# A two-layer attention and feed-forward kernel: the last block's normalised input transposed by DMA, its weights loaded once, exponentials written to PSUM

## The chip, the cores and the metric

The kernel runs on one core of a Trainium2 chip. The metric is the device time of one execution in microseconds. Before the change the median of three runs is 1620.17 us (1619.24 to 1620.29). A core has five engines that run their own instruction streams and meet at semaphores: TensorE (PE), VectorE (DVE), ScalarE (ACT), GpSimd (POOL) and SyncE (SP), which here only issues DMAs. Data lives in SBUF (128 partitions) and in eight PSUM banks that TensorE writes.

## The reference

There are 32 batches; each has x and a context of 128 rows by 1024. Four blocks are added to x one after the other:

```python
x = x + _L0_xattn_ref(_layernorm(x), ctx, ctx)      # autocorrelation through FFTs, top 9 of 128 lags, softmax
x = x + _L0_ffn_ref(_layernorm(x), W_base, ...)     # 1024x1024 base product + 8 LoRA experts of rank 16, top 2
x = x + _L1_xattn_ref(_layernorm(x), ctx, ...)      # 8 heads over a sliding window of 16
x = x + _L1_ffn_ref(_layernorm(x), A, B, Wr)        # 4 LoRA experts of rank 16, top 2, no base product
```

The fourth block, which the change touches most, is

```python
logits = flat @ Wr.T
topk_vals, topk_idx = jax.lax.top_k(logits, 2)
gates = softmax(logits where they are in the top 2, else -inf)
mid = jnp.einsum('tf,erf->ter', flat, A)
delta = jnp.sum(gates[:, :, None] * jnp.einsum('ter,eor->teo', mid, B) * 4.0, axis=1)
```

## The kernel before

**Stages.** `mk_kernel` walks over the 32 batches (line 964). For each it calls `load_batch` (stage `load`), `autocorr` for each half of 512 columns (stages `spec`, `corr`, `top`, `wt`, `inv`), `ffn0` (`ffn0`, `gate`, `base`), `attention` (`kv`, `q`, `S`, `PV`, `wo`) and `ffn1`. A stage works on tiles of 128 x 512 fp32 in SBUF (`U()`, 43 buffers named `u`) and on PSUM banks of the same shape (`B()`, eight named `p`). Products that need more than 16 bits take each operand as a pair of fp16 numbers, high part and remainder, and sum three matmuls (`THREE`, line 429); `pair(U())` holds such a pair in one `u` buffer.

**The fourth block before.** `ffn1` (line 932) calls `ln`, which takes mean and variance from row sums that `wo` left (`stats`: two squares on ACT, a power on POOL) and returns `normalise(g)`, one activation from x to a new `u` buffer. `transposed` (line 787) turns the normalised half with four TensorE transposes of 128 x 128 fp32 into a PSUM bank. An ACT activation writes the high fp16 part of it, a DVE subtraction the remainder. Twelve matmuls per half against `ar4` (128 x 68) give the low-rank product and the router's logits. `ffn0` uses `transposed` in the same way and keeps it.

**Weights.** `prep_ffn` scales every weight by its largest absolute value. For the base weights, before took a bound in its place: it loaded the 16 pieces of 128 x 512, multiplied each 128 x 128 part with itself on TensorE, summed all in one bank, took the sum of the diagonal and its square root on POOL. Then it loaded the 16 pieces a second time (`load_w`) and `pieces` made the pairs `wsp`, in turns by "P" (high part on POOL, remainder on DVE) and "V" (high part on ACT, remainder on DVE).

**The softmax of the lags.** In `autocorr` the correlations stand in a PSUM bank `pc`. Four activations (lines 758 and 759) write exp(pc - max) to a `u` buffer; a DVE instruction keeps the top 9 of each row.

**What sets the order.** Nothing is issued as it is called. `Planner` records each operation (a group of matmuls is one), works out what depends on what through its tiles, and estimates a duration (`_cost`). `plan` then places the operations one by one on the five engines: whenever an engine is free in the plan's own clock, the ready operation with the lowest value of `T * batch - tail - bias[stage]` goes next, where `tail` is the estimated work that hangs on it. Buffers are handed out in that order; a bound on how many batches are open (`win`), reserves of buffers (`su`, `sp`, `ru`, `rp`) and `margin` hold operations back. `emit` writes the instructions out in the planned order, so that every engine's order is fixed in the program, and on the chip an engine waits at an instruction until its operands are there. All instructions therefore carry one line in the profile, L363, and are told apart by their tiles. A DMA's semaphore is one of eight that SP uses in turn; SP waits for the DMA eight before.

Of the kernel before, what the change touches and what calls it, by code (L numbers as in the profile page):

```python
# [27 lines left out]
TINY = 1e-30  # L28
CFG = {'nu': 43, 'nd': 2, 'en': 'G', 'cl': 'G', 'xl': 'G', 'sm': 'V', 'sw': 'A', 'wg': 'PV', 'gram': 1, 'q0': 'G', 'ns': 28, 'nt': 48, 'phases': ((0.0, {'T': 19.75, 'margin': 43, 'win': 5, 'su': 4, 'sp': 0, 'ru': 1, 'rp': 0, 'bias': {'kv': -4.7, 'load': 9.8, 'S': -5.8, 'gate': 42.6, 'ffn1': 24.9, 'q': 1.0, 'top': 0.7, 'PV': -5.5, 'inv': 3.0, 'wt': 9.9, 'spec': 6.0, 'wo': 18.7, 'ws': -16.0, 'base': -2.4, 'ffn0': 56.2, 'corr': 7.7, 'setup': -2.3}}),)}
NTOP = int(2 * math.log(S))  # L30
# [75 lines left out]
class Planner:  # L106
# [72 lines left out]
    def _cost(self, op, method, v, kw):  # L179
# [27 lines left out]
        elif eng == "DVE":  # L207
            n = max(n, size(src))
            two = method in ("tensor_copy", "tensor_scalar", "memset") and not psum and n > 64
            op.dur += 6 * n / 0.96 + 67 if method == "reciprocal" else (n * (0.5 if two else 1.0) + 64 + 59 * nsc) / 0.96  # L210
            op.dur += 70.0 * ("accum_out" in v) + {"match_replace": 67.0, "transpose": 25.0}.get(method, 0.0)
        elif eng == "Pool":
            small = mybir.dt.size(out.proto.dtype) == 2
            if method == "memset":
                op.dur += 40.0 + (0.85 if small else 0.2) * n
            else:
                rate = 1.2 if method == "tensor_scalar" else 1.88 if small else 2.1
                if any(x.proto.ap[-1][0] == 0 for x in v.values()) and n > 128:
# [14 lines left out]

    def plan(self, phases, stop=None):

# [11 lines left out]
        for t in tiles:  # L247
            t.index = None
        for o in reversed(ops):
            o.tail = o.dur + max((s.tail + self._lat(o, s) for s in o.succs  # L250
                                  if s.batch == o.batch or o.batch < 0 and s.batch <= 0), default=0.0)
# [24 lines left out]
        while events:  # L276
            now = events[0][0]
            if stop is not None and now > stop:
                break
            if phases and now >= phases[0][0]:  # L280
# [3 lines left out]
            while events and events[0][0] <= now:  # L284
# [14 lines left out]
                for s in o.succs:  # L299
                    s.ready = max(s.ready, now + self._lat(o, s))  # L300
                    s.wait -= 1
# [8 lines left out]
            for e in self.ENGINES:  # L310
                if busy[e] > now:
                    continue
                for i, (_, o) in enumerate(ready[e]):
# [17 lines left out]
                    order.append(o)  # L331
                    end = now + o.dur
                    busy[e] = now + o.cold if e == "SP" else end
# [18 lines left out]
        self.order = order  # L352
        if stop is None and len(order) < len(ops):
            return None
        return now

# [8 lines left out]

def plan_args(c):
    scarce = lambda f: {"u": f["su"], "p": f["sp"], "d": 9, "m": 3, "r": 9, "s": 9, "t": 9}
    reserve = lambda f: {"u": f["ru"], "p": f["rp"], "m": 1, "s": 4, "t": 6}
    return [(t * 1e3, (f["T"] * 1e3, f["win"], f["margin"] * 1e3, scarce(f), reserve(f),
                       {k: v * 1e3 for k, v in f["bias"].items()})) for t, f in c["phases"]]  # L370


@with_exitstack
def mk_kernel(ctx: ExitStack, tc: tile.TileContext, T: dict, out: bass.AP):
# [23 lines left out]
    def U():  # L398
        return P.tile("u")
# [39 lines left out]
    G.memset(mhalf, -0.5)  # L439
    half = const("half", [128, 1])  # L440
    G.memset(half, 0.5)

# [79 lines left out]
    def prep_ffn():  # L522
        mx, m5 = P.fixed(slot("wmx", [128, 32])), P.fixed(slot("wm5", [128, 5]))
        absmax = lambda o, i, ax=AX.X: V.tensor_reduce(o, i, axis=ax, op=ALU.max, apply_absolute_value=True)

        def load_w(k):
            t = U()
            SP.dma_start(out=t, in_=T["wbT"][k // 2 * 128 : (k // 2 + 1) * 128, k % 2 * HALF : (k % 2 + 1) * HALF])
            return t

        def load_ar(name, i, w, rows):
# [15 lines left out]
        if CFG["gram"]:  # L547

            V.scalar_tensor_tensor(M(), p[:, 0:128], 1.0, ident, op0=ALU.mult, op1=ALU.mult, accum_out=mx[:, 1:2])
            V.tensor_scalar(mx[:, 2:3], mx[:, 1:2], TINY, None, op0=ALU.add)  # L550
            G.tensor_tensor(mx[:, 0:1], mx[:, 2:3], half, op=ALU.pow)
        for i in range(4):
# [7 lines left out]
        for i, (lo, hi) in enumerate(((0, 1 if CFG["gram"] else 16), (16, 20), (20, 24), (24, 26), (26, 28))):  # L560
            V.tensor_reduce(m5[:, i : i + 1], mx[:, lo:hi], axis=AX.X, op=ALU.max)
# [83 lines left out]
    def ln(src, sums):  # L645
# [10 lines left out]
        return normalise  # L656

    def gates(vals, E, pex, tl, sc, fac, imm):

# [67 lines left out]
    def autocorr(b, hf, normalise, x, c16, ksc, sums):  # L727
# [236 lines left out]
    for b in range(NB):  # L964
# [7 lines left out]
        ffn1(b, x, sums)  # L972
    P.plan(plan_args(CFG))
    with tc.manual_schedule():
# [79 lines left out]
```

## Time and profile before

| | us |
|---|---|
| median of three runs | 1620.17 |
| profiled execution | 1620.67 |
| its span | 1618.9 |
| PE busy | 1539.9 |
| DVE busy | 1467.7 |
| ACT busy | 1407.4 |
| POOL busy | 1369.9 |
| DMA queue q1, share of 16 engines | 49.5% |

The profiled execution's time is its span, from the first instruction to the last, and 1.8 us around it. Busy times are sums over an engine's instructions, and a row of the profile reads: engine, operation, output <- inputs by tile name, shape, count, then busy time and the mean duration of one in nanoseconds, then the engine's idle time just before such instructions and who ended it. The mean of one matmul is longer than its share of the engine, because matmuls overlap; busy time over count is nearer to what one costs. From about 600 to 1450 us the profile repeats itself batch by batch.

### The profile page before, as it was taken

What the parts mean: (1) busy time and instruction counts of PE and PEld (TensorE: products, weight loads), DVE (VectorE), ACT (ScalarE), POOL (GpSimd) and SP (SyncE); (2) the same over time, 40 slices, a digit from 0 to 9 for tenths busy, and PEclk for the clock granted to TensorE, in tenths of its full rate; (3) what the DMA queues carried; (4) which work ended last, traced back from release to release, by engine and by line L of the source; (5) the groups of instructions that cost most, each with busy time, mean ns of one, the idle gap of its engine ahead of it and who ended that gap; (6) DMA issues with size and microseconds to landing.
All of it is one profiled execution on the core that took longest, in us unless ns stands there. A gap on an engine that the chain in (4) does not pass through costs nothing.

```text
span 1618.9 us, 52341 instructions
## 1 busy us (share of the span) xinstructions
PE 1539.9 (95%) x19272; PEld 1012.6 (63%) x19272; DVE 1467.7 (91%) x5037; ACT 1407.4 (87%) x2817; POOL 1369.9 (85%) x1508
## 2 busy tenths in 40 slices
PE   5589999999999999999999999999999999999974
PEld 4345666666666666666666666666666666666653
DVE  5978999999999999999999999999999999999774
ACT  5698989998999989999999999999999999998752
POOL 6888879899798898988889998888899888889741
PEclk9889999999999999999999999999999999999986
DMA  7713545554554545544455555455555445554441
GB/s 248 216 47 46 91 76 98 92 101 79 107 97 65 96 94 99 96 97 92 65 95 93 100 98 96 91 73 86 95 99 104 89 90 80 79 98 71 64 59 42
DMA packets 856928, 149.96 MB, mean 93 GB/s; under 512 B 808480, under 2 KB 810784, under 8 KB 856672
## 3 DMA queue, kind: packets, MB, share of 16 engines
q1 hardware_dynamic: 856672, 146.61, 49.5%
q8 instruction: 153, 2.51, 0.7%
q14 instruction: 103, 0.84, 0.2%
HBM read 45.99 MB, written 16.78 MB: 39 GB/s over the span
## 4 chain that ended last, share of the span: by engine, by line
PE 58%; ACT 19%; DVE 8%; POOL 6%; issue 6%; DMA 2%; SPq 0%; ACTq 0%; POOLq 0%; DVEq 0%
PE p L363 58%; ACT u L363 17%; DVE u L363 5%; POOL vpad L363 3%; POOL u L363 2%; DVE s L363 2%; DMA u<-in_wbT 1%; POOL t L363 1%; ACT vpad L363 1%; DVE t L363 1%; DVE wsp L363 1%; DVE mm L363 1%; SPq L363 0%; ACT p L363 0%; DMA u<-u 0%
## 5 line engine op out<-in xcount | busy, mean ns | idle before, releaser
L363 POOL TENSOR_TENSOR u<-u,u 128x512 f32<-128x512 f32 (+1 forms) x640 | 772.0, 1234 | 122.7 <-ACT u L363 114.9
L363 PE MATMUL p<-wsp,u 128*128 128x512 f16 (+1 forms) x2304 | 408.7, 327 | 1.7 <-DVE u L363 0.9
L363 ACT ACTIVATE u<-p 64x512 f32<-64x512 f32 (+1 forms) x576 | 328.6, 589 | 73.9 <-PE p L363 62.3
L363 ACT ACTIVATE u<-p,t 128x128 f32<-128x128 f32 (+4 forms) x704 | 335.4, 532 | 34.6 <-PE p L363 21.2
L363 ACT ACTIVATE u<-u,t 128x512 f32<-128x512 f32 (+1 forms) x448 | 312.2, 721 | 39.9 <-DVE u L363 16.6
L363 PEld LDWEIGHTS <-u 128*128 128x128 f16 x3072 | 220.7, 98 | 175.5 <-issue 4.0
L363 DVE SCALAR_TENSOR_TENSOR u<-p,u 128x512 f32<-128x512 f32 (+1 forms) x448 | 291.1, 677 | 37.6 <-PE p L363 24.3
L363 PE MATMUL p<-u,ch 128*128 128x512 f16 x960 | 237.5, 380 | 0.4 <-DVE u L363 0.4
L363 PEld LDWEIGHTS <-qbd 128*128 128x128 f16 x6144 | 173.6, 96 | 29.4 <-issue 10.8
L363 PEld LDWEIGHTS <-vbd 128*128 128x128 f16 x6144 | 164.7, 97 | 31.1 <-issue 27.0
L363 PE MATMUL p<-u,vbd 128*128 128x32 f16 x6144 | 166.3, 177 | 11.4 <-ACT u L363 7.8
L363 PE MATMUL p<-k,qbd 128*128 128x32 f16 x6144 | 175.0, 177 | 0.4 <-issue 0.4
L363 ACT ACTIVATE u<-u,t,t 128x512 f32<-128x512 f32 x192 | 146.8, 815 | 20.4 <-POOL t L363 12.4
L363 PEld LDWEIGHTS <-ch 128*128 128x128 f16 x960 | 90.7, 100 | 102.9 <-issue 13.6
L363 PE MATMUL p<-ident,u 128*128 128x128 f32 x768 | 107.3, 280 | 30.7 <-ACT u L363 25.7
L363 POOL TENSOR_TENSOR u<-u,s 128x512 f32<-128x512 f32 x128 | 133.1, 1051 | 1.0
L363 ACT ACTIVATE u<-u 128x512 f16<-128x512 f32 x194 | 116.1, 628 | 13.1 <-DVE u L363 9.3
L363 PEld LDWEIGHTS p<-ident,u 128*128 128x128 f32 x768 | 87.9, 142 | 59.5 <-ACT u L363 40.6
L363 PE MATMUL p<-u,cf 128*128 128x512 f32 x256 | 119.1, 603 | 0.7 <-POOL u L363 0.7
L363 DVE SCALAR_TENSOR_TENSOR u<-p,t,u 128x256 f32<-128x256 f32 (+1 forms) x192 | 103.6, 555 | 13.7 <-ACT u L363 13.0
L363 POOL TENSOR_TENSOR vpad<-u,vpad 128x512 f16<-128x512 f32 x64 | 100.5, 1575 | 10.1 <-ACT vpad L363 10.0
L363 POOL TENSOR_TENSOR t<-t,mhalf 128x1 f32<-128x1 f32 x128 | 73.0, 571 | 40.8 <-DVE t L363 40.6
(160 smaller groups left out, 2818.5 us busy)
## 6 DMA issues: line engine op xcount, KB each, us to landing
vbd<-d SPq DMA_DIRECT2D x256, 128.0 KB
u<-u SPq DMA_DIRECT2D x192, 128.0 KB
u<-in_ctx SPq DMA_DIRECT2D x64, 256.0 KB
u<-in_x SPq DMA_DIRECT2D x64, 256.0 KB
qbd<-u SPq DMA_DIRECT2D x512, 32.0 KB
out<-u SPq DMA_DIRECT2D x64, 256.0 KB
u<-in_wbT SPq DMA_DIRECT2D x32, 256.0 KB
u<-u SPq DMA_DIRECT2D x64, 126.0 KB
```

The lines of the kernel that those rows point to most:

```text
L363: fn(*[f(a) for a in args], **{k: f(a) for k, a in kw.items()})
```

## The change

`ffn1` no longer transposes on TensorE. A new function `turned` takes the statistics, computes the normalised half twice on ACT (once in fp32, once as the high fp16 part), subtracts them on POOL to the remainder, and `turn` issues one DMA in transposing mode from SP for the pair: 128 x 1024 fp16 in SBUF to eight turned 128 x 128 blocks in another `u` buffer, which the twelve matmuls of that half read. `prep_ffn` loads the base weights once, keeps the 16 buffers, takes the largest absolute values on DVE, and splits them by "V" and "G" (high part and a scaled fp32 copy on ACT, remainder on POOL) in turns. In `autocorr` the exponentials overwrite `pc` in PSUM. The planner's settings are new: other priorities and reserves, a second set of them from 1447 us of the plan's clock on, and a constant added to each DMA's estimated duration; POOL's cost of a scaling with 16-bit output is estimated higher. With these the order of nearly all instructions changes.

```diff
-CFG = {... 'wg': 'PV', 'gram': 1, 'q0': 'G', 'ns': 28, 'nt': 48, 'phases': ((0.0, {'T': 19.75, 'margin': 43, 'win': 5, 'su': 4, 'sp': 0, 'ru': 1, 'rp': 0, 'bias': {...}}),)}
+CFG = {... 'wg': 'VG', 'q0': 'G', 'ns': 28, 'nt': 48, 'plan': {'phases': [{'at': 0.0, 'T': 21.78, 'margin': 26, 'win': 5, 'su': 10, 'sp': 99, 'ru': 1, 'rp': 0, 'bias': {...}}, {'at': 1447.0, 'T': 22.55, 'margin': 20, 'win': 6, 'su': 6, 'sp': 99, 'ru': 3, 'rp': 0, 'bias': {...}}], 'slack': [1.0, 0, 274.653]}}
...
-                rate = 1.2 if method == "tensor_scalar" else 1.88 if small else 2.1
+                rate = (2.8 if small else 1.2) if method == "tensor_scalar" else 1.88 if small else 2.1
...
+        stretch, wait, land = slack
+        lat = lambda a, b: self._lat(a, b) + (wait if a.eng != b.eng else 0.0)
+        dur = lambda o: o.dur if o.eng == "PE" else o.dur + (land if o.batch >= 0 else 0.0) if o.eng == "SP" else o.dur * stretch
...
-        p = B()
+        wb = []
         for k in range(16):
-            t = load_w(k)
-            if not CFG["gram"]:
-                absmax(mx[:, k : k + 1], t)
-                continue
-            with P.group():
-                for j in range(4):
-                    c = t[:, j * 128 : (j + 1) * 128]
-                    PE.matmul(p[:, 0:128], lhsT=c, rhs=c, start=k == 0 and j == 0, stop=k == 15 and j == 3)
...
+            t = U()
+            SP.dma_start(out=t, in_=T["wbT"][k // 2 * 128 : (k // 2 + 1) * 128, k % 2 * HALF : (k % 2 + 1) * HALF])
+            absmax(mx[:, k : k + 1], t)
+            wb.append(t)
...
-            pieces([wsp[:, r, k // 2, lo : lo + HALF] for r in range(2)], load_w(k), 0, CFG["wg"][k % len(CFG["wg"])])
+            pieces([wsp[:, r, k // 2, lo : lo + HALF] for r in range(2)], wb[k], 0, CFG["wg"][k % len(CFG["wg"])])
...
+    def turned(src, sums):
+
+        nm, rs = stats(src, sums)
+        r32, nb = s(1), s(1)
+        G.tensor_scalar(r32, rs, 32.0 * X_SC, None, op0=ALU.mult)
+        G.tensor_tensor(nb, nm, r32, op=ALU.mult)
+
+        def half(g):
+            xn, t, tT = U(), pair(U()), pair(U())
+            A.activation(xn, src[g], AF.Identity, bias=nb, scale=r32)
+            A.activation(t[:, 0], src[g], AF.Identity, bias=nb, scale=r32)
+            G.tensor_tensor(t[:, 1], xn, t[:, 0], op=ALU.subtract)
+            turn(tT, t)
+            return tT
+
+        return half
...
+    def turn(dst, src):
+
+        SP.dma_start(out=dst.rearrange("p i (j n) -> p (i j) n", n=128), in_=src.rearrange("p i n -> p (i n)"), transpose=True)
...
+        for j in range(4):
+            A.activation(pcv[:, j, :], pcv[:, j, :], AF.Exp, bias=nm[:, j : j + 1])
         e = U().rearrange("p (j t) -> p j t", t=128)
-        for j in range(4):
-            A.activation(e[:, j, :], pcv[:, j, :], AF.Exp, bias=nm[:, j : j + 1])
-        V.scalar_tensor_tensor(e, r1, NEG, e, op0=ALU.is_equal, op1=ALU.mult)
+        V.scalar_tensor_tensor(e, r1, NEG, pcv, op0=ALU.is_equal, op1=ALU.mult)
...
-        normalise, ph = ln(x, sums), B()
-        for g in range(2):
-            p, t16 = transposed(normalise, g), pair(U())
-            A.activation(t16[:, 0], p, AF.Copy, scale=32.0 * X_SC)
-            V.scalar_tensor_tensor(t16[:, 1], p, 32.0 * X_SC, t16[:, 0], op0=ALU.mult, op1=ALU.subtract)
+        half, ph = turned(x, sums), B()
+        for g in range(2):
+            t16 = half(g)
```

More of the change, by code (lines that the diff above doesn't have):

```diff
@@ L28 @@
 TINY = 1e-30
-CFG = {'nu': 43, 'nd': 2, 'en': 'G', 'cl': 'G', 'xl': 'G', 'sm': 'V', 'sw': 'A', 'wg': 'PV', 'gram': 1, 'q0': 'G', 'ns': 28, 'nt': 48, 'phases': ((0.0, {'T': 19.75, 'margin': 43, 'win': 5, 'su': 4, 'sp': 0, 'ru': 1, 'rp': 0, 'bias': {'kv': -4.7, 'load': 9.8, 'S': -5.8, 'gate': 42.6, 'ffn1': 24.9, 'q': 1.0, 'top': 0.7, 'PV': -5.5, 'inv': 3.0, 'wt': 9.9, 'spec': 6.0, 'wo': 18.7, 'ws': -16.0, 'base': -2.4, 'ffn0': 56.2, 'corr': 7.7, 'setup': -2.3}}),)}
+CFG = {'nu': 43, 'nd': 2, 'en': 'G', 'cl': 'G', 'xl': 'G', 'sm': 'V', 'sw': 'A', 'wg': 'VG', 'q0': 'G', 'ns': 28, 'nt': 48, 'plan': {'phases': [{'at': 0.0, 'T': 21.78, 'margin': 26, 'win': 5, 'su': 10, 'sp': 99, 'ru': 1, 'rp': 0, 'bias': {'kv': -25.3, 'load': 11.2, 'S': -5.0, 'gate': 236.5, 'ffn1': 51.9, 'q': 45.5, 'top': 0.2, 'PV': -10.3, 'inv': 3.1, 'wt': 15.3, 'spec': 11.1, 'wo': 137.4, 'ws': -5.6, 'base': -3.1, 'ffn0': 59.0, 'corr': 1.3, 'setup': 18.5}}, {'at': 1447.0, 'T': 22.55, 'margin': 20, 'win': 6, 'su': 6, 'sp': 99, 'ru': 3, 'rp': 0, 'bias': {'kv': -38.3, 'load': 17.0, 'S': -7.4, 'gate': 291.2, 'ffn1': 41.4, 'q': 59.7, 'top': 12.3, 'PV': -5.2, 'inv': 29.0, 'wt': 4.4, 'spec': -20.3, 'wo': 151.8, 'ws': 6.4, 'base': -1.8, 'ffn0': 82.1, 'corr': 7.6, 'setup': -12.8}}], 'slack': [1.0, 0, 274.653]}}
 NTOP = int(2 * math.log(S))
@@ L232, in _lat, with plan @@
         return self.LAT[a.eng] + (120.0 if b.eng == "PE" else 0.0)
-    def plan(self, phases, stop=None):
+    def plan(self, phases, slack):
         ops, tiles = self.ops, {}
@@ L248, in plan @@
             t.index = None
+        stretch, wait, land = slack
+        lat = lambda a, b: self._lat(a, b) + (wait if a.eng != b.eng else 0.0)
+        dur = lambda o: o.dur if o.eng == "PE" else o.dur + (land if o.batch >= 0 else 0.0) if o.eng == "SP" else o.dur * stretch
         for o in reversed(ops):
-            o.tail = o.dur + max((s.tail + self._lat(o, s) for s in o.succs
+            o.tail = dur(o) + max((s.tail + lat(o, s) for s in o.succs
                                   if s.batch == o.batch or o.batch < 0 and s.batch <= 0), default=0.0)
@@ L277, in plan @@
             now = events[0][0]
-            if stop is not None and now > stop:
-                break
             if phases and now >= phases[0][0]:
@@ L299, in plan @@
                 for s in o.succs:
-                    s.ready = max(s.ready, now + self._lat(o, s))
+                    s.ready = max(s.ready, now + lat(o, s))
                     s.wait -= 1
@@ L331, in plan @@
                     order.append(o)
-                    end = now + o.dur
+                    end = now + dur(o)
                     busy[e] = now + o.cold if e == "SP" else end
@@ L352, in plan @@
         self.order = order
-        if stop is None and len(order) < len(ops):
-            return None
-        return now
+        return now if len(order) == len(ops) else None
     def emit(self):
@@ L366, in plan_args @@
 def plan_args(c):
+    us = lambda v: v * 1e3
     scarce = lambda f: {"u": f["su"], "p": f["sp"], "d": 9, "m": 3, "r": 9, "s": 9, "t": 9}
     reserve = lambda f: {"u": f["ru"], "p": f["rp"], "m": 1, "s": 4, "t": 6}
-    return [(t * 1e3, (f["T"] * 1e3, f["win"], f["margin"] * 1e3, scarce(f), reserve(f),
-                       {k: v * 1e3 for k, v in f["bias"].items()})) for t, f in c["phases"]]
+    return [(us(f["at"]), (us(f["T"]), f["win"], us(f["margin"]), scarce(f), reserve(f),
+                           {k: us(v) for k, v in f["bias"].items()})) for f in c["phases"]], c["slack"]
 @with_exitstack
@@ L439, in mk_kernel @@
     G.memset(mhalf, -0.5)
-    half = const("half", [128, 1])
-    G.memset(half, 0.5)
     ch = load("ch", dt=F16).rearrange("p (m i n) -> p m i n", m=4, i=2)
@@ L524, in prep_ffn @@
         absmax = lambda o, i, ax=AX.X: V.tensor_reduce(o, i, axis=ax, op=ALU.max, apply_absolute_value=True)
[L526 to L529, printed above, removed]
         def load_ar(name, i, w, rows):
@@ L534, in load_ar @@
             return t
-        p = B()
+        wb = []
         for k in range(16):
-            t = load_w(k)
-            if not CFG["gram"]:
-                absmax(mx[:, k : k + 1], t)
-                continue
-            with P.group():
-                for j in range(4):
-                    c = t[:, j * 128 : (j + 1) * 128]
-                    PE.matmul(p[:, 0:128], lhsT=c, rhs=c, start=k == 0 and j == 0, stop=k == 15 and j == 3)
[L547 to L551, printed above, removed]
+            t = U()
+            SP.dma_start(out=t, in_=T["wbT"][k // 2 * 128 : (k // 2 + 1) * 128, k % 2 * HALF : (k % 2 + 1) * HALF])
+            absmax(mx[:, k : k + 1], t)
+            wb.append(t)
         for i in range(4):
@@ L559, in prep_ffn @@
             absmax(mx[:, 26 + i : 27 + i], t[:, :, 64:68], AX.XY)
-        for i, (lo, hi) in enumerate(((0, 1 if CFG["gram"] else 16), (16, 20), (20, 24), (24, 26), (26, 28))):
+        for i, (lo, hi) in enumerate(((0, 16), (16, 20), (20, 24), (24, 26), (26, 28))):
             V.tensor_reduce(m5[:, i : i + 1], mx[:, lo:hi], axis=AX.X, op=ALU.max)
@@ L972, in mk_kernel @@
         ffn1(b, x, sums)
-    P.plan(plan_args(CFG))
+    P.plan(*plan_args(CFG["plan"]))
     with tc.manual_schedule():
```

## The prediction

> **What bounds the kernel now.** I read the page's totals first, then the busy time in windows of one batch, then the chain of waits inside one window, and then the instruction rows that the change touches.
>
> ```profile
> PE 1539.9 (95%) x19272; PEld 1012.6 (63%) x19272; DVE 1467.7 (91%) x5037; ACT 1407.4 (87%) x2817; POOL 1369.9 (85%) x1508
> ```
>
> TensorE is the fullest, but the other three stand within 11% of it, so the average alone does not say what a gain on TensorE is worth. The windows (length; busy time of PE, PEld, DVE, ACT, POOL; granted clock; DMA share; GB/s) say more:
>
> ```profile
> 0.00:47.00 47.00, 30.03 (x190) 25.56 (x191) 29.17 (x121) 29.80 (x55) 31.28 (x45) 0.93 0.74 234
> 47.00:94.00 47.00, 25.16 (x118) 13.52 (x117) 43.94 (x144) 30.11 (x63) 37.47 (x36) 0.75 0.56 171
> ...
> 840.45:887.50 47.05, 46.90 (x599) 30.63 (x599) 44.31 (x156) 43.18 (x88) 42.05 (x47) 1.00 0.53 91
> ```
>
> In the middle one batch takes 47.05 us and PE works 46.90 of it: there TensorE's own work is the time. The start loses 39 us of PE in 94; the stretch from 1502.7 to the end, asked in the same way, has 87.0 of PE in 116.2. The chain of waits repeats every 47.05 us, and it crosses from the matmuls through DVE, ACT and POOL back to a transpose of `ffn1`:
>
> ```profile
> 840.45 27.25 PE p L363 x308
> ...
> 887.49 0.33 PE p L363
> ```
>
> PE's instructions in order of time:
>
> ```profile
> 84.90 1.12 PE L363 MATMUL p<-ident,u 128*128 128x128 f32 x4 [15.94 <-ACT u L363]
> ...
> 879.60 1.02 PE L363 MATMUL p<-u,woT 128*128 128x512 f32 x2
> ...
> 887.49 0.33 PE L363 MATMUL p<-ident,u 128*128 128x128 f32 x1 [0.15 <-ACT u L363]
> ```
>
> The second product with `woT` at 879.60 gives the row sums that `ffn1` needs; its first transpose starts 7.89 us later, having waited 0.15 us for the normalised x. This chain is the one to watch. The rows whose prices I use:
>
> ```profile
> L363 PE MATMUL p<-ident,u 128*128 128x128 f32 x768 | 107.3, 280 | 30.7 <-ACT u L363 25.7 <-POOL u L363 3.0
> ...
> L363 POOL TENSOR_TENSOR u<-u,u 128x512 f16<-128x512 f32 x256 | 293.1, 1163 | 101.9 <-ACT u L363 101.5
> ...
> L363 ACT ACTIVATE u<-u,t,t 128x512 f32<-128x512 f32 x192 | 146.8, 815 | 20.4 <-POOL t L363 12.4 <-DVE wmx L363 6.2 <-DVE t L363 1.6
> ...
> L363 ACT ACTIVATE u<-p 128x512 f16<-128x512 f32 x192 | 102.1, 586 | 4.1 <-PE p L363 3.2
> ```
>
> **Transposes off TensorE.** 8 of a batch's 24 go. In the same list eight of them start at 870.10 and the next matmul at 870.97, 0.87 us later, 0.109 us each; busy time over count is 0.140. 256 of them are 27.9 to 35.8 us of PE; I take 0.112, the value nearest the dense middle: -28.7 us, 0.9 a batch.
>
> **Where their work goes.** ACT loses the PSUM eviction (102.1/192 = 0.53 us) and gains a second normalisation from SBUF (146.8/192 = 0.76): +0.47 us a batch. DVE loses two subtractions from PSUM (their row: 121.3 us busy for 192, 0.63 each): -1.3. POOL gains two, fp16 out (293.1/256 = 1.145), and one scaling of a column (about 0.2): +2.5. One batch in the middle then asks for PE 46.0, POOL 44.5, ACT 43.7, DVE 43.0. PE stays longest, but its lead over the next falls from 2.6 to 1.5 us.
>
> **The transposing DMA.** No row of before shows one, so I bound how long it takes (L, issue to usable) and count how much time the order gives it. In the order of the built program PE has, between `wo`'s second product of batch b and the first `ffn1` matmul of b: that product 0.86, eight products with `cf` 1.78, eight transposes 0.87, three products of `spec` 0.65, two `S` groups 2.86, two `gate` groups 1.42, five `base` groups of 1.29 and one transpose: 15.0 us. The chain needs 7.9 us to the first normalised half (above), 0.2 for the extra POOL column, 0.8 for the second normalisation, 1.16 for POOL's subtraction: 10.1. So the first DMA has 4.9 us. The second half comes 1.6 us later by ACT and is read one `base` group and twelve matmuls (1.66 us) later: also 4.9.
> L from below: four 128 KB copies `u<-u` and the eight small `qbd` copies are issued on SP at these rates,
>
> ```profile
> 866.81 6.11 SPq L363 DMA_DIRECT2D qbd<-u  x8
> ...
> 873.22 2.48 SPq L363 DMA_DIRECT2D u<-u  x4
> ```
>
> and in the chain of waits of the start:
>
> ```profile
> 23.29 4.25 DMA u<-u
> ```
>
> Two thirds of that (an estimate for the quiet middle) is the low end, 2.8 us. The high end takes the 256 KB as runs of 32 bytes, as `qbd` is written: 32 KB each 0.76 us, so 6.1 us, plus about 2 for a first landing: 8. I take 4.3, at the `u<-u` row, since source rows are 2 KB as there: in time with 0.6 to spare. Past 4.9 every microsecond is paid once a batch, because `wo`, the chain and `ffn1` form a loop through PE's order: about 29 us per us of L. As L may now and then exceed its share I enter +3 us.
>
> The Trainium skill speaks against the move: "VectorE: DVE Perf Modes", sections on the three transpose paths and the rules, prices a 128x128 16-bit transpose at 390 ns on TensorE and 1309 ns by DMA, and says to use TensorE where PSUM will do. Eight such blocks would be an estimated 10.5 us, 5.6 too late, and the sum about 1765. "DMA: Bandwidth & Descriptors", "Latency and other measured facts", gives 261 GB/s for a transposing DMA, by which 256 KB move in an estimated 1.0 us and the sum is the one below. No run here shows either yet.
>
> **SP's queue.** Per batch SP issues 38 DMAs, whose issue times in that window add up to some 29 of 47 us; two more, priced like `u<-u` or `qbd` (0.6 to 0.8 us), are 1.5. Behind the first transpose's wait for POOL stand six `qbd` copies of the next batch, and `S` reads those. Cost taken: nothing, covered by the 18 us that SP has free; if one issue took 3 us instead, the `qbd` copies would come 4.5 us late and `S` would wait some 2 us a batch, 60 in all.
>
> **The start.** Sixteen loads of 256 KB and 64 products of the sum of squares (17.9 us of PE, which stands idle there anyway) go; 16 maxima on DVE (0.66) come, 8 fewer fp16 subtractions on DVE (15.7/16 = 0.98), 16 more activations (0.70). The wait of 15.94 us at 84.90 covers the second loading and splitting; I expect half of it to go. Against this, the new order puts more ACT work early: summing rows over the order, ahead of batch 0's first `ffn1` matmul stand ACT 149.5, POOL 146.3, DVE 145.0, PE 110.6 us, where before had 135.7, 144.8, 142.4 and 128.7. That matmul ran at 188.0, 43.2 after the largest sum. After: 149.5 + 43.2 - 8 = 185 (175 to 195).
>
> **Exponentials in PSUM.** 256 activations now write PSUM. Their row is 0.381 us; the PSUM-to-PSUM rows of 8 and 4 columns (0.318, 0.344) neither forbid a change nor give one: -0.05 to +0.05 each, 13 us of ACT either way over the run, not on the path while ACT has 2 us free a batch. DVE's product reads PSUM, 0.680 for 0.747. The bank is held one DVE step longer, but two banks a batch are no longer taken by transposes. Taken as nothing.
>
> **End.** In the last batch the step from normalised x to the first `ffn1` matmul ran 1605.67 to 1608.20, 2.5 us; now 0.8 + 1.16 + 4.3 = 6.3 less a waiting transpose: +3.
>
> **The sum,** against the profiled execution (1620.67 us, its span 1618.9 and 1.8 around it; 0.5 above the median 1620.17). After batch 0's `ffn1`, before had 1373.9 us of PE work in 1430.9; the new order has 1349.5, 24.4 less. Span: 185 + 1430.9 - 24.4 + 3 (end) + 3 (late DMAs) + 4 (the thinner lead over POOL, 0.3%) = 1601.5; with the 1.8, 1603 us, 1.1% faster.
>
> **Rivals.**
> 1. The DMA comes late, L over 4.9. For it: no row shows one, it waits behind two `qbd` copies, and 8192 short writes are eight `qbd`s. Against: the plain copies of its size land in time. L = 6.5 costs 1.6 x 29 = 46: 1649; L = 8 costs 90: 1693. It passes no change at L = 5.5.
> 2. POOL or ACT becomes the bound. For: POOL at 44.5 of 46.0 with two subtractions that must sit at the right places. Against: DVE ran 44.3 beside PE's 46.9 without costing PE more than 0.15. If PE loses 0.6 a batch: 1620.
> 3. The new order is worse at the start: 16 of 43 `u` buffers hold weights until the scale is known, and more ACT work stands early. 20 us lost there instead of 3 gained: 1626.
>
> **Chances.** Forecast 0.57, rival 1 0.27, rival 2 0.08, rival 3 0.08. The forecast's own range is 1583 to 1617. Under 1580 needs the whole 15.94 us hole and no late DMA; over 1665 needs L over 7, about a third of rival 1: low 1580, high 1665. Below 0.2% (3.2 us) this kernel can't be told from no change: faster 0.59 (forecast, a little of rival 2), same 0.07, slower 0.34.
>
> **What will show it.** One batch in the middle near 46.1 us with PE 45.9 busy; no wait of PE on a DMA of `u` before the `ar` matmuls; if that wait appears, its length times 29 is the loss. POOL near 1445, ACT 1433, DVE 1427 busy. The first `ffn1` matmul near 185. An issue of the transpose on SP above 1 us, or `S` waiting for `qbd`, would show the queue. The prediction is wrong if L exceeds 5.5 or the start loses more than 20.

## The result and the profile after

The changed kernel takes 1626.26 us (median of six runs, 1623.01 to 1628.76), the one before 1619.91 in the same comparison: 1.0036 times as long, with a 95% interval of 1.0023 to 1.0049. It is slower, by 0.36%, where 1.1% faster was forecast. The profiled execution took 1626.28 us, its span 1624.5.

The page's totals, the three windows of the prediction and its row of `ident` transposes, now of the kernel after:

```profile
PE 1515.3 (93%) x18888; PEld 967.5 (60%) x18888; DVE 1447.9 (89%) x4978; ACT 1443.0 (89%) x2833; POOL 1429.8 (88%) x1602
```

```profile
0.00:47.00 47.00, 14.45 (x46) 8.20 (x46) 35.18 (x145) 23.51 (x46) 27.09 (x43) 0.79 0.72 226
47.00:94.00 47.00, 35.15 (x152) 17.16 (x152) 42.19 (x121) 45.64 (x87) 39.83 (x38) 0.85 0.37 107
900.00:947.00 47.00, 46.62 (x604) 30.10 (x601) 44.16 (x154) 44.15 (x88) 43.84 (x50) 1.00 0.58 103
```

```profile
L363 PE MATMUL p<-ident,u 128*128 128x128 f32 x512 | 80.6, 280 | 7.5 <-ACT u L363 4.9 <-POOL u L363 2.2
```

The instructions have moved as the diff says: 8 of 24 transposes a batch are gone from TensorE, whose busy time fell by 24.6 us. The time did not follow. To see where it went I compare the 16 middle batches of both kernels (from the first `ar` matmul of batch 10 to that of batch 26; the columns are those of the windows above), before first:

```profile
655.12:1408.27 753.15, 750.73 (x9570) 490.49 (x9569) 708.98 (x2481) 690.53 (x1393) 672.83 (x736) 1.00 0.51 91
```

```profile
654.35:1410.75 756.40, 743.40 (x9441) 478.19 (x9440) 702.75 (x2449) 706.77 (x1393) 701.27 (x785) 1.00 0.57 102
```

A batch went from 753.15/16 = 47.07 us to 47.28, while PE's work in it went from 46.92 to 46.46. Before, PE was idle for 2.4 us in 16 batches; after, for 13.0. The row of the `ar` matmuls, asked for these 16 batches alone, names what it was idle for (behind the second bar: idle time before them, and what ended it):

```profile
L363 PE MATMUL p<-ar,u 128*128 128x68 f16 x384 | 17.4, 195 | 11.5 <-DMA u<-u 11.3
```

The chain of waits through one batch of the kernel after begins and ends with that DMA:

```profile
936.55 4.46 DMA u<-u
...
941.05 25.99 PE p L363 x333
...
983.28 5.81 DMA u<-u
```

PE's and then SP's instructions in order of time around it show which of the two halves is late, and why:

```profile
923.20 1.02 PE L363 MATMUL p<-u,woT 128*128 128x512 f32 x2
...
938.93 0.54 PE L363 MATMUL p<-ar,u 128*128 128x68 f16 x12
939.31 1.46 PE L363 MATMUL p<-wsp,u 128*128 128x512 f16 x6
941.05 0.55 PE L363 MATMUL p<-ar,u 128*128 128x68 f16 x12 [0.29 <-DMA u<-u]
```

```profile
932.46 1.38 SPq L363 DMA_DIRECT2D qbd<-u  x2
934.14 1.36 SPq L363 DMA_TRANSPOSE u<-u  x1
935.55 0.91 SPq L363 DMA_DIRECT2D qbd<-u  x1
936.55 1.54 SPq L363 DMA_TRANSPOSE u<-u  x1
```

The first half (938.93) runs without a wait; the second, one `base` group later, waits. Its DMA could be issued only after SP had spent 1.36 us on issuing the first and 0.91 on a `qbd` copy that stands between them. Over the whole run the first halves wait 0.5 us in sum before the last batch, the second halves 24.2 (added up from the starts of PE's instructions). Issue times on SP (min/median/max in ns) and, in the list of DMAs, the median time from issue to landing (the trace gives a landing for 31 of the 64, nearly all of them second halves):

```profile
L363 SPq DMA_TRANSPOSE u<-u x64: 1242/1433/2551, 178.0 to 1611.3; - x64
```

```profile
u<-u SPq DMA_TRANSPOSE x64, 4.4
```

### The profile page after: what moved, and what is told of

Same layout as the page of the kernel before. It is cut to its first block, busy times and chain, and to the rows that moved or that the text cites. A ratio compares the mean times of both kernels' runs of the same rounds, so it can differ in the third digit from the quotient of the medians.

```text
span 1624.5 us, 51576 instructions
## 1 busy us (share of the span) xinstructions
PE 1515.3 (93%) x18888; PEld 967.5 (60%) x18888; DVE 1447.9 (89%) x4978; ACT 1443.0 (89%) x2833; POOL 1429.8 (88%) x1602
## 4 chain that ended last, share of the span: by engine, by line
PE 48%; ACT 27%; DMA 11%; DVE 6%; issue 4%; POOL 3%; SPq 0%; ACTq 0%; POOLq 0%; DVEq 0%
PE p L363 48%; ACT u L363 25%; DMA u<-u 9%; POOL u L363 3%; DVE s L363 3%; DVE u L363 2%; ACT p L363 1%; DMA u<-in_wbT 1%; DVE m L363 1%; DVE wsp L363 0%; DVE t L363 0%; DMA u<-in_x 0%; SPq L363 0%; DMA vbd<-d 0%; DMA u<-in_bl 0%
## 5 line engine op out<-in xcount | busy, mean ns | idle before, releaser
L363 POOL TENSOR_TENSOR u<-u,u 128x512 f32<-128x512 f32 (+1 forms) x704 | 847.3, 1230 | 93.8 <-ACT u L363 80.9
L363 ACT ACTIVATE u<-p 64x512 f32<-64x512 f32 (+1 forms) x512 | 302.6, 592 | 22.0 <-PE p L363 6.7
L363 ACT ACTIVATE u<-p,t 64x512 f32<-64x512 f32 (+2 forms) x448 | 274.3, 621 | 37.5 <-PE p L363 29.0
L363 DVE SCALAR_TENSOR_TENSOR u<-p,u 128x512 f32<-128x512 f32 (+1 forms) x384 | 256.9, 682 | 32.6 <-ACT u L363 16.2
L363 PE MATMUL p<-u,ch 128*128 128x512 f16 x960 | 257.1, 385 | 4.3 <-POOL u L363 1.9
L363 ACT ACTIVATE u<-u,t,t 128x512 f32<-128x512 f32 (+1 forms) x256 | 194.5, 815 | 5.1 <-POOL t L363 4.1
L363 PE MATMUL p<-u,cf 128*128 128x512 f32 x256 | 129.3, 606 | 3.1 <-POOL u L363 3.0
L363 ACT ACTIVATE u<-p,t,t 128x512 f32<-128x512 f32 x128 | 98.5, 774 | 0.0
L363 DVE TENSOR_REDUCE s<-u 128x16 f32<-128x512 f32 x128 | 87.3, 682 | 10.6 <-ACT u L363 9.0
L363 DVE STREAM_TRANSPOSE u<-u 128x512 f32<-128x512 f32 x128 | 89.3, 698 | 6.5 <-POOL u L363 6.3
```

What stands on the lines that cost most here:

```text
L363: fn(*[f(a) for a in args], **{k: f(a) for k, a in kw.items()})
```

## The experiments

Three places can hide what is looked for: the DMA itself, SP's queue, and the engines behind it. Whenever the code changes, the planner works out a new order. So all runs but the first keep the order of the kernel after, save where an edit below moves a DMA on SP. Where an instruction is replaced or left out, the plan is made as if nothing had changed, and the other instruction is put in when it is written out (`other` below):

```diff
             for fn, args, kw in o.calls:
+                fn = getattr(o, "other", fn)
                 fn(*[f(a) for a in args], **{k: f(a) for k, a in kw.items()})
```

"A batch" below is always the length of the 16 middle batches over 16, in the one traced execution of each run; the times are medians of all executions, with the ratio to the kernel before and its 95% interval.

### Back on TensorE, with a new order (e4_back_on_pe)

```diff
-        half, ph = turned(x, sums), B()
+        normalise, ph = ln(x, sums), B()
         for g in range(2):
-            t16 = half(g)
+            p, t16 = transposed(normalise, g), pair(U())
+            A.activation(t16[:, 0], p, AF.Copy, scale=32.0 * X_SC)
+            V.scalar_tensor_tensor(t16[:, 1], p, 32.0 * X_SC, t16[:, 0], op0=ALU.mult, op1=ALU.subtract)
```

> The changed kernel with the transposes of layer 1's feed-forward back on TensorE (normalised fp32, transpose, eviction as fp16 and subtraction on DVE, as before); weights loaded once, exponentials in PSUM and the new settings of the order stay. The order is worked out anew with 1488 us of work for PE, where before had 1503 and after 1460. Theory A (moving the transposes is what costs, since it gained nothing and the start gained 6): about before's batch of 47.05 us and after's start, 1612 to 1618. Theory E (the new order's settings cost something by themselves): 1624 or more.

1744.27 us, 1.0774 (1.0757 to 1.0790). Theory E's side, by far more than it priced. In the built programs of before and after, the settings of the planner (biases by stage, periods) give one order that repeats from batch to batch; here no two batches have the same, and waits are spread over all engines (between 600 and 1400 us, POOL's instructions on `m` wait 38.2 us for DVE's `t`, up to 7.2 at once). The run says nothing of the transposes. It says that a part of this change can't be undone while the planner is left to rework the order, and so the other runs hold it fixed.

### The transposing DMA itself (e1_copy_both, e2_copy_second)

In the same order, both DMAs (or, with a flag, only that of `g == 1`) are plain copies:

```diff
-        SP.dma_start(out=dst.rearrange("p i (j n) -> p (i j) n", n=128), in_=src.rearrange("p i n -> p (i n)"), transpose=True)
+        SP.dma_start(out=dst.rearrange("p i (j n) -> p (i j) n", n=128), in_=src.rearrange("p i (j n) -> p (i j) n", n=128))
```

> The changed kernel, in the same order on every engine, with both transposing DMAs of each batch turned into plain copies of the same 256 KB between the same buffers (left out: the transposition, so layer 1's feed-forward multiplies untransposed numbers). Theory A (the second transposing DMA comes late): its matmuls waited 24.2 us in sum for it; plain copies are issued in about 0.6 us instead of 1.4 and land in about 2.7 us, so that wait goes and nothing else changes: 1626 - 24 = 1602, up to 1608 if a fifth of it returns elsewhere. Theory B (POOL and ACT, now at 44 of 47 us a batch, are the bound): the wait goes from the DMA to POOL and ACT, and the time stays above 1618.

> As the run before, but only the second half's DMA is a plain copy; the first stays a transposing one (left out: the transposition of the second half). Theory A: the first was in time, the second was issued 13.3 us after wo's second product and read 16.7 to 16.8 us after it by the order; a plain copy that lands in 2.7 us is ready at 16.0, so the whole gain is there already: 1602 to 1609. Theory C (what costs is SP's time, 1.4 us for each issue, that makes later qbd copies late): half the issue time stays, so about half the gain: 1612 to 1616. Theory B: above 1618.

Both: 1614.88 us, 0.9977 (0.9967 to 0.9986), 46.92 a batch. Second alone: 1620.98, 1.0008 (0.9998 to 1.0017), 46.89 a batch. The first lies between the theories' numbers, the second above all that theory A allows, where theory B put it. But theory B's reason, that the wait goes over to POOL and ACT, is not what the rows show: a good part of it stays with the DMA. Theory A had the copies' landing wrong. Of the run with both, the list of DMAs and the row of `ar` in the 16 batches, then that row of the run with the second alone:

```profile
u<-u SPq DMA_DIRECT2D x192, 128.0 KB, 2.6
...
u<-u SPq DMA_DIRECT2D x64, 256.0 KB, 4.8
```

```profile
L363 PE MATMUL p<-ar,u 128*128 128x68 f16 x385 | 17.6, 195 | 5.0 <-DMA u<-u 4.9
```

```profile
L363 PE MATMUL p<-ar,u 128*128 128x68 f16 x384 | 17.4, 195 | 5.1 <-DMA u<-u 4.7
```

A plain copy of the same 256 KB at the same place takes 4.8 us to land, no less than the transposing one with its 4.4. I had taken 2.7, from the 128 KB copies that are issued elsewhere. What the plain copy saves is issue time: the second is issued 12.77 us after `wo`'s second product (mean of the 16 batches) where the transposing one came at 13.67, and the wait shrinks from 11.3 to 4.9 us. Of what is left, 4.1 us stand before the first half, which had waited for nothing: the first plain copy, issued at 11.16 where the transposing one was at 11.12, now lands too late in some batches. With the second alone a plain copy, it is issued at 13.67 as before, and the matmuls that read it start 4.20 us after that, not 4.63; its issue alone is 0.9 us shorter (0.60 for 1.49). So no run shows a cost of the transposition beyond its issue, and what counts is the moment of issue.

### SP's queue (e8_adjacent, e9_two_between)

On SP alone, the `qbd` copy between the two DMAs is put behind the second (e8), or one more is put between (e9, the same loop with the next `q` copy moved ahead):

```diff
         self.order = order
+        sp = [i for i, o in enumerate(order) if o.eng == "SP"]
+        turns = [k for k, i in enumerate(sp) if order[i].calls[0][2].get("transpose")]
+        for j, k in reversed(list(zip(turns[0::2], turns[1::2]))):
+            for i in reversed(sp[j + 1 : k]):
+                if order[i].stage == "q":
+                    order.insert(sp[k], order.pop(i))
```

> The changed kernel with the whole computation, and the same order on PE, DVE, ACT and POOL; on SP alone the qbd copy that stood between the two transposing DMAs of a batch is issued behind the second. Theory A: the second is issued about 0.9 us earlier, and nearly the whole wait of 0.89 us a batch goes, save in the batches where it lands in over 5 us: 1605 to 1611. Theory C: the qbd copies behind are no earlier, and the one moved is later: 1624 to 1630. Theory D (two transposing DMAs side by side take each other's bandwidth, so the second lands as late as before): 1623 to 1627.

> The changed kernel with, on SP alone, one more qbd copy put between the two transposing DMAs of a batch (the next one in SP's order; two stand between instead of one). Theory A (the wait before the second half is set by what SP issues and moves between the two): none between gave 1613.5 and one gave 1626; with two the second transposing DMA is issued 0.7 to 0.9 us later, PE has no slack left to hide it, and the wait grows by that much in each of some 29 batches: 1646 to 1652. Theory H (the gain of the run with none between came from an accident of timing): no such step, 1620 to 1632.

None between: 1613.5 us, 0.9967 (0.9955 to 0.9978), 2.5 us above the range of theory A and far below those of C and D, which fall. The `ar` row of the 16 batches, and SP's queue:

```profile
L369 PE MATMUL p<-ar,u 128*128 128x68 f16 x384 | 17.3, 194 | 0.2 <-DMA u<-u 0.2
```

```profile
925.37 1.39 SPq L369 DMA_DIRECT2D qbd<-u  x2
927.04 2.92 SPq L369 DMA_TRANSPOSE u<-u  x2
930.01 5.41 SPq L369 DMA_DIRECT2D qbd<-u  x6
```

Two between: 1661.98 us, 1.0265 (1.0250 to 1.0280), more than the 1646 to 1652 expected. The order in which copies and scores meet changes with it, and some scores of this kernel are computed from other queries than they should be; its end is 6.8 us longer as well, which is no part of the dose. The row:

```profile
L369 PE MATMUL p<-ar,u 128*128 128x68 f16 x385 | 18.2, 197 | 24.5 <-DMA u<-u 24.4
```

The three kernels with none, one and two copies between stand in a row. Means of the 16 batches, from `wo`'s second product: the second DMA is issued at 12.75, 13.67 and 14.49 us, and the matmuls that read it start at 17.44, 18.30 and 19.12. With one or two between, they start 4.63 us after the issue, both times; with none they start where PE's order puts them (15.74 for the first half and 1.67 for the groups between), and the data is there. The batch takes 46.70, 47.28 and 48.38 us: the first 0.86 us of delay costs 0.58, the next 0.82 costs 1.10 (in the mean: with two between, single batches run from 46.9 to 51.7). That is the cause of the loss, shown in both directions.

It is not all of the missing gain: 46.70 is 0.37 less than before, and 0.9 was forecast.

### What holds the batch at 46.70 (e10 to e16)

All of these start from e8_adjacent. First POOL, since `p<-cf,u` now waits for it at the start of each batch: its two subtractions to DVE (e10, the line below), or only that of `g == 1` (e14), or, in place of it, `P.ops[-1].more = 3 * g`, by which POOL adds `ident` to `ident` three times into a spare tile that nothing reads (e11).

```diff
             G.tensor_tensor(t[:, 1], xn, t[:, 0], op=ALU.subtract)
+            P.ops[-1].other = nc.vector.tensor_tensor
```

> The kernel with the two transposing DMAs side by side (1613.5 us), and the two subtractions that make the low fp16 half carried out by DVE instead of POOL, at the same place in the written order. POOL has 2.3 us a batch less (43.8 to 41.5), DVE some 1.3 more (43.8 to 45.1). Theory F (what is left of the missing gain, about 0.5 us a batch, is PE waiting at the products with cf for a POOL whose queue is full): those waits go, 1597 to 1604. Theory G (they come from ACT or from the order, or a fuller DVE takes POOL's place): 1611 to 1625.

> The kernel with the two transposing DMAs side by side (1613.5 us), and three additions of 128x128 on POOL behind the second subtraction of each batch, which nothing reads: an estimated 1.2 us more of POOL a batch (43.8 to 45.0 of 46.7). Theory F (POOL's queue sets the waits at the products with cf): what stands behind comes later and half to all of it reaches PE, 0.6 to 1.2 us in 29 batches: 1631 to 1648. Theory G (POOL has room, its 3 us of idle time take it up): 1612 to 1617.

> The kernel with the two transposing DMAs side by side (1613.5 us), with only the second half's subtraction on DVE at the same place in the order: POOL 1.16 us a batch less, DVE about 0.65 more. With both on DVE the matrix m that PE reads ahead of the first ar products came 0.8 us late. Theory F: POOL's relief is worth more than DVE's load, 1603 to 1612. Theory I: DVE's chain through m is as tight as POOL's queue, so some 0.3 us a batch is lost: 1615 to 1625.

Both on DVE: 1629.72 us, 1.0064 (1.0049 to 1.0079), 47.34 a batch, worse than either theory had it. One: 1617.02, 0.9984 (0.9975 to 0.9994), 46.85, as theory I said. More for POOL: 1644.08, 1.0150 (1.0134 to 1.0167), 47.81, as theory F said. PE's new wait in the first is DVE's `m`, in the last POOL's `u`:

```profile
L370 PE MATMUL p<-ident,m 128*128 128x128 f32 x32 | 10.2, 318 | 11.5 <-DVE m L370 11.5
```

```profile
L369 PE MATMUL p<-ident,u 128*128 128x128 f32 x256 | 40.2, 279 | 19.7 <-POOL u L369 19.5
```

Three additions of 0.399 us (1.2 us) cost 1.11 a batch. So neither DVE nor POOL has anything to give. That adding costs does not yet mean that taking away gains; the three edits below are e12, e15 and e16, one in each:

```diff
             G.tensor_tensor(t[:, 1], xn, t[:, 0], op=ALU.subtract)
+            P.ops[-1].other = lambda o, a, c, op: nc.gpsimd.memset(o, 0.0)
...
                 split(hi, lo, t, G)
+                if i:
+                    P.ops[-1].other = lambda o, a, c, op: nc.gpsimd.memset(o, 0.0)
...
                 G.tensor_scalar(rc, rc, W_SC, None, op0=ALU.mult)
+                P.ops[-1].other = nc.vector.tensor_scalar
```

> The kernel with the two transposing DMAs side by side (1613.5 us), in which POOL writes zeros into the low fp16 half instead of subtracting (left out: the low half of layer 1's normalised x, so its products keep only the high part). POOL has an estimated 1.8 us a batch less, no other engine has more, and the low half no longer waits for ACT. Adding 1.2 us to POOL cost 1.1 us a batch, so POOL's queue is on the loop that sets the batch. Theory F (POOL alone holds the batch above PE's own work): the waits at the products with cf (0.5 us a batch) go and the time falls to 1595 to 1603. Theory I (PE's order, POOL, ACT and DVE are tied within a few tenths, as moving the subtractions to DVE suggests, which cost 16): under half of that, 1607 to 1614.

> The kernel with the two transposing DMAs side by side (1613.5 us), in which POOL writes zeros into the low fp16 half of v instead of subtracting, twice a batch (left out: the low half of v in layer 0's attention). These stand in the stretch in which POOL runs without a gap from the softmax sums that it gets from DVE to the u that the products with cf read; the subtractions that the earlier run took away stand ahead of that stretch, and taking them gained nothing. An estimated 1.5 us a batch less of POOL. Theory F2 (that stretch of POOL sets the waits at cf, 0.52 us a batch): 46.2 us a batch and 1597 to 1603. Theory I (everything is tied, another engine comes up at once): above 1608.

> The kernel with the two transposing DMAs side by side (1613.5 us) and the whole computation; the scaling of the softmax reciprocals (128x16, four a batch, 0.24 us each on POOL) is done by DVE in the same place. POOL loses 0.96 us a batch in its stretch without gaps, DVE gains an estimated 0.4. Theory F2: most of the 0.5 us a batch goes, 1598 to 1606. Theory I: DVE takes the place, 1610 to 1618.

Zeros for the low half of x: 1611.4 us, 0.9959 (0.9945 to 0.9973), 46.69 a batch. Zeros for that of v: 1609.34, 0.9940 (0.9923 to 0.9958), 46.68. The scaling on DVE: 1622.05, 1.0014 (1.0005 to 1.0023), 47.14, worse than either theory had it: one more load on DVE. The first two take 1.3 us a batch from POOL and leave the mean of the steady batches as it was (their few us come from the first batches and the end); theories F (1595 to 1603 us) and F2 (46.2 a batch) fall. POOL's instructions in the first show where the time went: POOL now waits for DVE's `t` and `s` instead, and goes on as late as before.

```profile
1062.32 0.99 POOL L662 MEMSET u<- 128x512 f16 x2
1063.27 0.57 POOL L370 TENSOR_TENSOR t<-t,mhalf 128x1 f32<-128x1 f32 x1
1065.91 0.45 POOL L370 TENSOR_TENSOR m<-mm,t 128x36 f32<-128x36 f32 x2 [2.08 <-DVE t L370]
...
1068.04 0.48 POOL L370 TENSOR_SCALAR s<-s 128x16 f32<-128x16 f32 x2 [1.39 <-DVE s L370]
```

The mean of the second hides two kinds of batches. Eight of its 16 take 46.4 us, where none in e8 takes less than 46.55; the other eight take 46.5 to 47.4. In six of these PE waits again, before the scores (which read the `qbd` copies) or before `ar`, 0.2 us a batch over all 16. The two rows:

```profile
L370 PE MATMUL p<-k,qbd 128*128 128x32 f16 x3072 | 87.3, 176 | 1.5 <-issue 0.9 <-DMA qbd<-u 0.5
...
L370 PE MATMUL p<-ar,u 128*128 128x68 f16 x384 | 17.3, 194 | 1.7 <-DMA u<-u 1.7
```

So relief of POOL at that place did shorten single batches by 0.28, and waits that end with DMAs, as far as the rows name them, took much of it back. ("issue" means that the profile names nothing that ended the wait.)

### ACT, and what comes behind it (e17 to e20)

The chain of waits of e8_adjacent through one batch runs neither through POOL's long queue nor through DVE, but through ACT, and from ACT by way of two POOL steps into PE; the window of that stretch (PE, PEld, DVE, ACT, POOL busy) has ACT full:

```profile
1064.94 0.62 ACT u L369
1065.56 0.08 issue
1065.64 0.81 ACT u L369
...
1071.72 0.68 ACT vpad L369
1072.40 0.07 issue
1072.47 2.53 POOL vpad L369 x2
1075.00 1.00 POOL u L369
1076.00 0.04 issue
1076.05 23.70 PE p L369 x312
```

```profile
1055.97:1072.40 16.43, 16.34 (x198) 11.06 (x197) 16.22 (x78) 16.38 (x37) 13.89 (x22) 1.00 0.68 109
```

In that stretch stand the two fp32 normalisations of `turned`. Made by POOL in the same place (e17, below), or left out (e18: from e12_zeros, with `lambda *a, **k: None` in this place):

```diff
             A.activation(xn, src[g], AF.Identity, bias=nb, scale=r32)
+            P.ops[-1].other = lambda o, i, f, bias, scale: nc.gpsimd.tensor_scalar(o, i, scale, bias, op0=ALU.mult, op1=ALU.add)
```

> The kernel with the two transposing DMAs side by side (1613.5 us) and the whole computation; the fp32 normalised x, two a batch of 0.81 us each on ACT, is made by POOL at the same place in the order, where POOL stood idle for 1.8 us waiting for ACT. In the chain of waits of that kernel ACT runs 16.38 us out of 16.43 without a gap, from the heads of the batch to the low halves of k and v, before the chain goes on through POOL into PE. Theory J (that stretch of ACT, which the change made longer by its second normalisation, is what holds the batch at 46.7 instead of the 46.0 that was forecast): it becomes some 1.5 us shorter, until PE's own work of about 46.2 sets the batch, 1596 to 1604. Theory K (POOL, an estimated 1.0 us for each, then comes late at the transposing DMAs or behind them): 1614 to 1635.

> The kernel in which POOL writes zeros instead of the low half (1611.4 us), and ACT no longer makes the fp32 normalised x, which nothing reads there (left out: the low half of layer 1's normalised x, as in that kernel). ACT has 1.6 us a batch less and no engine more. Taking 1.3 us from POOL at this place gained nothing in the steady batch (46.69 us). Theory J (ACT's stretch sets the batch): 46.2 us a batch, 1594 to 1602. Theory I (all four tied, so that taking from any single one gains nothing): 1607 to 1613.

On POOL: 1609.38 us, 0.9932 (0.9919 to 0.9944), 46.54 a batch, the shortest 46.3. Left out: 1606.53, 0.9924 (0.9909 to 0.9939), 46.51. Both lie between the theories: what relief of POOL did not give in the mean (0.01 and 0.02 us a batch), relief of ACT gives, but the gain stops after 0.2 of the 0.5 us that theory J hoped for. One reason stands in PE's rows of e17: the scores wait 2.0 us in the 16 batches, where the kernel after had none and e8 had 0.1; that is 0.12 a batch.

```profile
L370 PE MATMUL p<-k,qbd 128*128 128x32 f16 x3072 | 87.2, 176 | 2.0 <-issue 1.9
```

That the `qbd` copies come late there, behind the two transposing DMAs, is likely but not shown. In the chain of e17 ACT's stretch is gone, and another stands there, POOL's:

```profile
1080.25 1.33 POOL u L370 x2
1081.57 1.17 issue
1082.74 2.51 POOL u L370 x2
...
1094.38 4.09 POOL u L370 x4
...
1101.08 1.16 PE p L370 x8
```

So the last pair of runs takes one addition of 1.25 us out of that stretch of POOL (`drop` is true in the autocorrelation for `hf == 1`), in e17 (e19) and in e8 (e20):

```diff
         G.tensor_add(u, u, up)
+        if drop:
+            P.ops[-1].other = lambda *a, **k: None
```

> The kernel with the two transposing DMAs side by side and the normalised x made by POOL (1609.4 us), in which one addition a batch on POOL is left out, the last of the stretch of 20 us in which POOL runs without a gap up to the products with cf (left out: the second half of the complex product of one autocorrelation of layer 0, so the lags chosen there are others). In that kernel's chain of waits ACT has gone (2.5%) and POOL's stretch stands in it (35%). Theory L (the holders come one behind the other: the DMA, then ACT's stretch, then this stretch of POOL, then PE's own work): 1.25 us less of POOL, the waits at the products with cf go, and the steady batch falls from 46.54 to about 46.1: 1594 to 1600. Theory I (a tie, nothing is gained by taking from one): 1606 to 1611.

> The same addition left out of the kernel with the two transposing DMAs side by side alone (1613.5 us), where ACT's stretch of 16.4 us without a gap stands in the chain of waits. Theory L: POOL is not the holder there; the waits at the products with cf go and come back as waits elsewhere, the steady batch stays within 0.1 us of 46.70 and the time within 4 us of 1613.5. Theory F2 (POOL's stretch before the products with cf sets the batch there too): 0.4 to 0.5 us a batch gained, 1599 to 1604.

From e8: 1612.8 us, 0.9961 (0.9947 to 0.9975), 46.71 a batch, as theory L said; F2 falls again. The waits at `cf` went (the row's mean is 275 ns, as before the change, where e8 has 281), and came back at the next transposes, this time ended by ACT (first e8's row, then two of e20):

```profile
L369 PE MATMUL p<-cf,u 128*128 128x128 f32 x256 | 35.4, 281 | 1.1
```

```profile
L370 PE MATMUL p<-cf,u 128*128 128x128 f32 x256 | 31.2, 275 | 0.0
...
L370 PE MATMUL p<-ident,u 128*128 128x128 f32 x256 | 40.1, 279 | 7.0 <-ACT u L370 5.7
```

From e17: 1608.93, 0.9933 (0.9918 to 0.9948), 46.57 a batch: nothing gained, theory I. So POOL's stretch alone does not hold e17 either. There the chain of waits is 86% PE and 12% ACT, and of PE's 8.1 us of idle time in the 16 batches 5.7 stand before the `ident` transposes, ended by ACT, and 2.0 before the scores; what each of these costs was not taken apart further.

## Why the prediction was wrong

**The sign came from one term.** The forecast was 1603, the median 1626.3: 23.3 us off. By the medians of the runs: 12.8 for the late second DMA (1626.3 to 1613.5 in e8), 4.1 for ACT's normalisation (to 1609.4 in e17), 6.4 left, which no relief that was tried gave back whole (the lowest run, e18, which leaves out the low half of x, took 1606.5). The second of these steps is less firmly ACT's: zeros for v, a relief of POOL, gave as much in time. No run separates what the new order costs by itself from what the moved transposes cost.

**The step that failed** is "The second half comes 1.6 us later by ACT and is read one `base` group and twelve matmuls (1.66 us) later: also 4.9." It let the data set the second issue. SP set it: SP is a queue, and before the second DMA stand the issue of the first and a `qbd` copy. Both are in the prediction, in the paragraph on SP's queue ("priced like `u<-u` or `qbd` (0.6 to 0.8 us)", "Cost taken: nothing"), but only as a load on SP and as a delay for `S`; rival 1 names the place ("it waits behind two `qbd` copies") and prices nothing for it. The issue was also undersized: 1.43 us, median, against 0.6 to 0.8. The second came 2.55 us after the first, not 1.6 (13.67 less 11.12). What to count is one moment: issued at 13.67, usable at 18.30, wanted at 17.41. The second DMA had 3.7 us, where the prediction gave it 4.9.

**The duration L was right.** 4.3 was taken and 4.4 measured, 4.63 in the mean from issue to first use, both under the 4.9 (the longest of the 16 batches 5.9), and rival 1's price of 29 us per microsecond holds as an order of size: 0.88 us late in the mean, 24.2 us of waits in the run. Taking them away gave only 12.8: the 16 middle batches became 9.2 us shorter for 11.5 us of waits, and in the traced executions the start and the end grew by 1.6 and 1.3. Rival 1 is what happened, through the issue and not through L; it had 0.27. The argument against it, "the plain copies of its size land in time", was empty: from SBUF to SBUF there was none of its size, and such a copy lands in 4.8 (4.2 where the second alone is one).

**The chain to the first half** was put at 10.1 us and is 11.1 (10.95 in most batches); it was in time, because PE was 0.7 later than its 15.0 as well, most of it at the products with `cf`, which held PE for 2.31 us where 1.78 was counted.

**Where the work goes.** Forecast for a batch: PE 46.0, POOL 44.5, ACT 43.7, DVE 43.0. In the 16 batches of the kernel after: PE 46.46, POOL 43.8, ACT 44.2, DVE 43.9; with the waits at `cf` gone PE's is 46.2 (e20) or 46.1 (e19). The totals were within 2%; the changes were less near (DVE 0.4 less for a forecast 1.3, ACT 1.0 more for 0.47, POOL 1.8 more for 2.5). The use of them was worse: "the thinner lead over POOL" was entered as +4 us from the gap between two averages, while ACT's +0.47, counted only in a mean, stands in a stretch of 16.4 us where ACT is 99.7% busy (in e8). A mean of 44 in 47 does not show that.

**The start** was forecast at 185 for batch 0's first `ffn1` matmul and came at 181.9 (188.0 before): better than forecast, inside its 175 to 195. Rival 3 did not happen. **The end**, +3, is +0.7 (from batch 28's first `ffn1` matmul: 116.2 before, 116.9 after).

**Exponentials in PSUM:** forecast -0.05 to +0.05 us for each of 256; 0.381 before, 0.335 after, at the good end, and DVE's product 0.679 for a forecast 0.680. One of the two rows quoted as PSUM to PSUM, that of 4 columns, reads `lg`, which lies in SBUF; nothing rested on it. No run took this part alone.

**The two estimates from pages.** By the Trainium skill's page "VectorE: DVE Perf Modes", section "The three transpose paths", eight blocks at 1309 ns would be an estimated 10.5 us; the traces show 4.4 for all eight, and a plain copy of that size in the same queue 4.8. The 1.0 us that was worked out from a bandwidth is under a quarter of what was measured, issue included. The Trainium skill's page "Advanced Engine Details and Errata", section "X-Bar Transpose (TRN2)", says that transposing DMAs are as fast as regular ones; the landings agree, the issue times do not (1.43 us against 0.53).

**What was asked for as evidence** showed it: "no wait of PE on a DMA of `u` before the `ar` matmuls" is what failed, and "An issue of the transpose on SP above 1 us" is what was there. The signs were the right ones; the sum priced them at 3 us and at nothing.

**A version that beats both.** e17_xn_pool computes all that the kernel after does, with the two transposing DMAs side by side on SP and the fp32 normalised x made by POOL: 1609.38 us, 0.68% faster than before and 1.04% faster than the change as it was made.

## What to carry to other kernels

A DMA's moment of use is issue plus landing, and the issue has a queue of its own: list what the issuing engine has ahead of it, with issue times, for each of a pair and not for the first alone. Then follow the loop that sets the period in the chain of waits, engine by engine: when four engines are within 6% of each other, one that is 94% busy on average can be full just in the stretch that the loop goes through, and what relief gains at one place can be lost again at the next wait. Look at single batches too, not only at their mean. When an order is planned, test by replacing instructions inside the given order; a new plan is another kernel.

## What I had not expected of the hardware

- Issuing a transposing DMA of 128x1024 fp16 from SBUF to SBUF took SP 1.24 to 2.55 us, median 1.43; a plain copy of the same size in the same place about 0.53 (0.56 mean). The landing, counted from the start of the issue, differed little: 4.4 us against 4.2 when issued at the same moment, and 4.8 where both were plain.
- Copies of 128 KB elsewhere in the batch land in 2.6 us, the plain 256 KB copy among `qbd` copies (32 KB each, in runs of 32 bytes) in 4.8; loads of 256 KB from `in_ctx` land in 2.6. So size alone does not explain it; that the neighbours in the queue do is my reading, not shown by a run of its own. The Trainium skill's page "DMA: Bandwidth & Descriptors", section "Queues, rings and completion order", says that each DMA engine takes the descriptors of a ring in order, which would fit.
- A `p<-cf,u` matmul's mean busy time was 275 ns without a wait and 281 with one (the row's total 31.2 and 35.4 us in 16 batches): part of a wait of PE is booked as busy time, so PE's busy total (46.46 a batch) overstates its own work (46.2 in e20, 46.1 in e19).
